# Criss-cross attention and a Fourier mixer: the transform along h by even and odd frequencies, and one more tap by DMA

## The chip, the cores and the metric

The kernel runs on one core of a Trainium2 chip. The metric is the device time of one execution in microseconds (us), lower is better. TensorE is called PE in the profile, its weight loads PEld, VectorE DVE, ScalarE ACT, GpSimd POOL and SyncE SP.

## The reference

The input x has 8 images of 128 by 128 pixels (h, w) with 64 channels, all float32. Layer 0 is criss-cross attention: a pixel attends to its column and to its row with one softmax over both. Layer 1 is a mixer with a two-dimensional Fourier transform, and then a depthwise convolution.

```
Q, K, V = x w_q + b_q, x w_k + b_k, x w_v + b_v            # 8, 8 and 64 channels
att = softmax(concat[energy_H (without itself), energy_W])
x   = gamma * (att_H V + att_W V) + x
h   = ln(x, g1, b1) w_te + b_te                            # 64 -> 128 channels
F   = fft2(h, axes=(h, w))
fc  = gelu(concat[Re F, Im F] w_fc + b_fc)                 # 256 -> 256
x1  = x + (Re ifft2(fc[:128] + i fc[128:])) w_tp + b_tp    # 128 -> 64
h2  = ln(x1, g2, b2) w_fe + b_fe                           # 64 -> 128
d   = gelu(depthwise_conv3x3(h2, w_dw) + b_dw)
out = x1 + d w_fp + b_fp                                   # 128 -> 64
```

Here ln subtracts the mean over the channels and divides by sqrt(var + 0.001).

## The kernel before, in words

The program has two stages, one after the other, which meet in DRAM. All tiles are float32.

**Attention.** An image is worked in eight tasks: four "H" tasks, each 32 columns w with h on the partitions, and then four "W" tasks, each 32 rows h with w on the partitions. Task n of 64 is `tasks[n]`. The loop over n runs a software pipeline: in step n, task n + 1 is turned by PE (`turn`, L348), projected (`queries`, `values`, L362 and L381) and its energies' maxima taken by DVE (L438); task n gets its exponentials from ACT (L444) and its first products with the values (`attend`, L403, copied out of PSUM by ACT in L409); task n - 1 gets the rest. The instructions of each engine run in the order written in this loop. An H task's result goes to `yh`, which PE transposes after the fourth H task (`across`, L584 and L585). A W task's result goes to `yw`, a tile for two W tasks of which there are two: tasks 0 and 1 of an image share one, tasks 2 and 3 the other, and the next image takes them again in turn.

From then on POOL works on a W task. `total` (L522 to L524) adds the two denominators after ACT's weights (`weigh`, L514 to L516); in step n + 2 `combine` merges both results into x (L541, L544) and sends x to DRAM (`x2`, L545). The layer norm of layer 1 begins here too, in `norm_step(n, part)`, which is called four times in each step. Parts 0 and 2 square half of a task's x on ACT (L559) and sum it on DVE (L560), parts 1 and 3 sum the squares (L562), all for the task m = n - 4. For m = n - 5, part 3 computes the inverse root on POOL (L89 to L105), and after every second W task POOL scales x into `yw`, reordered to channels by rows (L574), and a DMA from POOL's queue writes these 64 rows of the image to `xn[b]` in DRAM (L578). `xn[b]` has the layout w, half of the image, channel, row in the half. The last three tasks do these things on DVE and SP instead (`merger`, `store`).

```
                    (nc.sync if m >= N - 3 else nc.gpsimd).dma_start(out=xn[b][:, blk // 2, :, :], in_=z)
```

**Mixer.** `transforms(b)` and `mlp(b)` only add tasks to a planner, `Plan`. It has for every task an engine, a cost, what it comes after, buffers that it takes and frees ("slots", of which "mm" are four PSUM banks), and a due time; going through time with the costs, it gives to each engine the ready task that is due first. The steps of the instruction streams of PE, ACT, DVE and POOL are then in that order. Image b is due one `PERIOD` after image b - 1, so that the transforms of image b stand between the instructions of the convolution of image b - 1.

The transforms of an image are these. `along_w` (L798) multiplies each half of `xn` with the real table of the transform along w; the first 64 partitions of its result hold the rows of the first half, the others those of the second, and ACT keeps it in `at` (L807). `along_h(g)` (L816 to L823) transforms along h for a group of four frequencies of w (the list `GROUPS`, 17 groups): four matmuls for one frequency, each with 64 channels as weights, 128 rows as contraction and the 128-wide tables `cos`, `sin` or `nsin` as the moving side. They fill one PSUM bank, and ACT copies it to `f` in one instruction (`keep_h`, L828). `channels` (L838) applies w_fc, `bend` (ACT, L848) the gelu, `hermite` (POOL, L854) adds or subtracts, `project` (L878) applies w_tp, ACT keeps the result in `gt` (L887). `inverse_h` (L893 to L896) and `inverse_w` (L906) go back, and DVE adds to x (L914).

The convolution goes by 17 chunks k of 8 lines, the last of one line. POOL scales the lines (`xc`, L1039), PE turns them (L1073) and expands them (L1095), ACT keeps `h` (L1115). The nine taps of the 3 by 3 window are added in `acc`: ACT makes the first (L1130); some others are made as products by ACT (L1134, tile `pr`) and added by a DMA that accumulates (`gather`, L1138, issued on POOL's queue: pr<-pr adds a second product to the first, acc<-pr adds the sum to `acc`); DVE does the rest as a scalar_tensor_tensor each (`tap`, L1144). Then gelu by ACT (L1191), w_fp by PE (L1206), the add by DVE (L1211) and the store. How many products go by DMA is set here; even chunks have one and odd chunks two, and the last image has one in its even chunks, while its odd chunks are done as full matmuls (`pairs`, L1156).

```
PRODS = 3
BY_DMA, BY_DMA_LAST = (1, 2), 1
```

## Time and profile before

| | us |
|---|---|
| median of 3 runs | 3202.73 |
| lowest and highest | 3199.78, 3213.37 |
| the profiled execution, time | 3198.24 |
| its span, first to last instruction | 3196.4 |
| busy in the span: PE, PEld | 2915.1, 2144.6 |
| busy: DVE, ACT, POOL | 2486.9, 2096.0, 1636.0 |
| attention, from the start to the mixer's first matmul | 1275.5 |
| mixer, from there to the end | 1920.9 |

"Busy" is the time in which an engine executes, and overlapping PE instructions are counted once. The span is what the program spends between its first and its last instruction; the profiled execution's own time is 1.8 us more, and it lies 4.5 us below the median. A released wait is named after the instruction that came last by the profile; where several end together, the name may be that of a neighbour. A matmul of float32 leaves two records. Counts of engines over the whole span mix the two stages, so the stages are best read in windows of their own.

### The profile page before, as it was taken

How to read it: one execution, taken by the hardware profiler on the slowest of the kernel's cores; microseconds unless marked ns; L12 is line 12 of the kernel's file. 1: busy time of each engine (PE TensorE's matmuls, PEld its weight loads, DVE VectorE, ACT ScalarE, POOL GpSimd, SP SyncE). 2: the span in 40 equal slices, each digit the busy share in tenths (PEclk: the TensorE clock that was granted, in tenths of full speed). 3: DMA queues.
4: the chain of work that ended last, by engine and by line, in shares of the span. 5: the costliest groups of instructions: out<-in, count | busy, mean ns of one | idle time of the engine just before them, and what ended most of it. 6: DMA issues, size and time to landing. Idle time of an engine off the chain costs nothing.

```text
span 3196.4 us, 110388 instructions
## 1 busy us (share of the span) xinstructions
PE 2915.1 (91%) x50476; PEld 2144.6 (67%) x50476; DVE 2486.9 (78%) x2313; ACT 2096.0 (66%) x2744; POOL 1636.0 (51%) x1974
## 2 busy tenths in 40 slices
PE   7998898988888986999999999999999999999978
PEld 5877777777777776766666575675675675665644
DVE  4575747574747576819999999999999999999996
ACT  3665656565656654537868867767777777777754
POOL 1095959595959585424525516515525425435421
PEclk8999999999999998999999999999999999999989
DMA  6024242424243422242674664655745745745645
GB/s 175 23 96 121 96 130 99 121 95 121 101 132 104 122 95 104 99 159 50 134 172 89 157 144 85 170 117 93 182 105 108 176 96 111 178 94 100 120 90 100
DMA packets 227069, 372.71 MB, mean 117 GB/s; under 512 B 143401, under 2 KB 176812, under 8 KB 208044
## 3 DMA queue, kind: packets, MB, share of 16 engines
q0 software_dynamic: 37072, 188.39, 26.1%
q1 hardware_dynamic: 188764, 177.19, 19.7%
q8 instruction: 396, 6.49, 0.8%
q14 instruction: 69, 0.57, 0.1%
q10 hardware_dynamic: 768, 0.07, 0.0%
HBM read 170.96 MB, written 102.26 MB: 85 GB/s over the span
## 4 chain that ended last, share of the span: by engine, by line
PE 49%; DVE 29%; POOL 9%; issue 6%; DMA 4%; ACT 2%; SPq 0%; POOLq 0%; ACTq 0%; DVEq 0%
DVE acc L1144 16%; PE fcps L838 6%; PE yp L403 6%; PE e L433 4%; PE dps L906 4%; POOL xb L544 3%; PE yps L893 3%; PE yps L895 3%; DVE m L438 3%; PE vps L381 3%; PE tp L348 3%; DMA acc<-pr 3%; PE pq L362 3%; PE op L1206 3%; PE tpy L584 2%
## 5 line engine op out<-in xcount | busy, mean ns | idle before, releaser
L1144 DVE SCALAR_TENSOR_TENSOR acc<-h,pk,acc 128x1024 f32<-128x1024 f32 x840 | 1270.0, 1517 | 49.6 <-ACT acc L1130 28.1
L854 POOL TENSOR_TENSOR gs<-gl 128x512 f32<-128x512 f32 (+2 forms) x272 | 441.9, 1644 | 303.3 <-ACT gl L848 301.9
L838 PE MATMUL fcps<-f,pk 128*128 128x512 f32 (+2 forms) x1088 | 508.9, 598 | 0.2 <-ACT f L828 0.2
L438 DVE TENSOR_REDUCE m<-e 128x8 f32<-128x1024 f32 x256 | 300.6, 1211 | 211.5 <-PE e L433 211.3
L444 ACT ACTIVATE att<-e 128x1024 f32<-128x1024 f32 x256 | 259.7, 1024 | 170.2 <-PE e L433 166.3
L848 ACT ACTIVATE gl<-fcps,pk 128x1024 f32<-128x1024 f32 (+2 forms) x272 | 289.9, 1073 | 96.3 <-PE fcps L838 77.6
L1039 POOL TENSOR_TENSOR xc<-x,st 128x512 f32<-128x512 f32 x128 | 184.1, 1454 | 293.8 <-PE tpn L1073 117.1
L1138 POOL DMA_DIRECT2D acc<-pr x120 | 105.6, 880 | 443.4 <-DVE acc L1144 268.6
L403 PEld LDWEIGHTS yp<-v,att 128*64 128x64 f32 x8192 | 268.9, 143 | 87.3 <-issue 39.6
L433 PE MATMUL e<-kt,qt 32*128 32x128 f32 x4096 | 302.7, 291 | 25.4 <-DVE v L384 13.6
L838 PEld LDWEIGHTS fcps<-f,pk 128*128 128x128 f32 x1088 | 191.9, 193 | 196.2 <-issue 146.4
L403 PE MATMUL yp<-v,att 128*64 128x65 f32 x8192 | 296.8, 229 | 18.9 <-issue 17.3
L433 PE MATMUL e<-qt,kt 32*128 32x128 f32 x4096 | 300.1, 288 | 12.2 <-issue 10.1
L433 PEld LDWEIGHTS e<-kt,qt 32*128 32x128 f32 x4096 | 262.6, 194 | 38.1 <-DVE v L384 17.6
L433 PEld LDWEIGHTS e<-qt,kt 32*128 32x128 f32 x4096 | 258.6, 193 | 19.7 <-issue 13.1
L820 PE MATMUL fps<-tb,at 128*64 128x128 f32 x1008 | 200.4, 281 | 23.3 <-DVE ot L1211 23.3
L1134 ACT ACTIVATE pr<-h,pk 128x1024 f32<-128x1024 f32 x176 | 214.3, 1237 | 0.0
L878 PEld LDWEIGHTS gps<-pk,gs 128*64 128x64 f32 x4032 | 137.3, 144 | 108.7 <-issue 57.5
L1115 ACT ACTIVATE h<-hp,pk 128x512 f32<-128x512 f32 x254 | 156.4, 669 | 71.4 <-PE hp L1095 71.2
L384 DVE TENSOR_TENSOR v<-vps,bv 128x1024 f32<-128x1024 f32 x128 | 156.0, 1218 | 60.6 <-PE vps L381 60.6
L893 PE MATMUL yps<-tb,gt 128*64 128x128 f32 x1024 | 202.0, 279 | 0.6 <-ACT gt L887 0.6
L894 PE MATMUL yps<-tb,gt 128*64 128x128 f32 x1024 | 202.0, 279 | 0.0
(218 smaller groups left out, 7419.9 us busy)
## 6 DMA issues: line engine op xcount, KB each, us to landing
acc<-pr POOLq DMA_DIRECT2D x120, 512.0 KB, 5.4
xb<-in_x_dram SPq DMA_DIRECT2D x32, 1024.0 KB
xn<-xn SPq DMA_DIRECT2D x32, 1024.0 KB
x<-x SPq DMA_DIRECT2D x32, 1024.0 KB
x<-spread POOLq DMA_DIRECT2D x32, 1024.0 KB, 8.4
x<-xb POOLq DMA_DIRECT2D x30, 1024.0 KB, 4.9
out_dram<-ot SPq DMA_DIRECT2D x120, 256.0 KB
xn<-yw POOLq DMA_DIRECT2D x14, 2048.0 KB, 9.4
```

The lines of the kernel that those rows point to most:

```text
L403: nc.tensor.matmul(yq[z, q, j, :], lhsT=att[:, q, j, z], rhs=self.v[:, r, :], start=True, stop=True)
L433: nc.tensor.matmul(e[:, q, j, :], lhsT=left[rows, 4 * a + j, :], rhs=right[rows, 4 * a + j, :], start=not msk, stop=j == 3 or not msk,)
L438: nc.vector.tensor_reduce(new.mneg[:, 2 * k : 2 * k + 2, 4 * a : 4 * a + 4], e1, AX.X, ALU.max, negate=True,)
L444: nc.scalar.activation(att, e2, AF.Exp)
L820: nc.tensor.matmul(fps[0:64, n, :], lhsT=re, rhs=cos, start=True, stop=False)
L838: nc.tensor.matmul(ps[:, sgn, 0:n], lhsT=w[:, cols], rhs=fv, start=True, stop=not mean)
L848: nc.scalar.activation(gl[:, :, 0:n], ps[:, :, 0:n], AF.Gelu, bias=bfc[:, half : half + 1])
L854: nc.gpsimd.tensor_tensor(gs[:, 0:n], gl[:, 0, 0:n], gl[:, 1, 0:n], ALU.add if half == 0 else ALU.subtract)
L893: nc.tensor.matmul(yps[0:64, c, :], lhsT=gr, rhs=cosn, start=True, stop=False)
L894: nc.tensor.matmul(yps[64:128, c, :], lhsT=gi, rhs=cosn, start=True, stop=False)
L1134: nc.scalar.activation(pr, self.lines(k, t), AF.Identity, bias=zero, scale=wdw[:, t : t + 1])
L1144: nc.vector.scalar_tensor_tensor(out=a, in0=self.lines(k, t), scalar=wdw[:, t : t + 1], in1=a, op0=ALU.mult, op1=ALU.add)
```

## The change

The halves of an image are no longer stored as they are. `xn[b]` gets in its first half the sum and in its second the difference of rows h and h + 64. The first two W tasks of an image are written to both halves by one DMA whose source repeats. After the other two, two DMAs add them to the first half in DRAM, and ACT makes the negative in four parts (tile `zn`, three buffers), each of which a DMA adds to the second half. For the last image DVE forms both, and SP writes them.

In the mixer the even frequencies of h then need only the sums and the odd ones only the differences, each with 64 rows. `along_h` takes two groups of frequencies at once and works on 64 partitions at a time with tables 64 wide: eight matmuls for one frequency, in two PSUM banks, one for even and one for odd frequencies of h. ACT copies each bank's part by itself. The tables `cos`, `sin` and `nsin`, the offsets in `project` and the tables of the way back follow the new order of frequencies.

Besides, in every chunk but the small ones of all images but the last, two products go by DMA (before: in odd chunks), with four `pr` buffers for three; the calls of `norm_step` with parts 0 to 2 stand later in the step; ACT in place of DVE copies an H task's maxima (L481); and the planner's due times and costs have other values.

```
-PRODS = 3
-BY_DMA, BY_DMA_LAST = (1, 2), 1
-
-
-PERIOD, GROUP0, GROUP, BACK0, BACK = 262.0, -1.9, 10.3, 174.8, 4.3
-CHUNK0, CHUNK, STAY, LOADX = 18.2, 14.2, 0.1, -10.2
+PRODS = 4
+BY_DMA, BY_DMA_LAST = (2, 2), 1
+PERIOD, GROUP0, GROUP, BACK0, BACK = 265.1, -5.4, 9.7, 171.9, 4.7
+CHUNK0, CHUNK, STAY, LOADX = 16.0, 14.4, 0.1, -18.5
+ZN = 3
+DLAG, LATE = 6.9, 8.6
+AH = 0.33
...
-    full = 2.0 * np.pi * (np.outer(n, n) % P) / P
+
+    k = np.arange(64)
+    half = 2.0 * np.pi * np.concatenate([np.outer(k, 2 * k + z) % P for z in range(2)], axis=0) / P
+    freq = np.concatenate([2 * k, 2 * k + 1])
+    full = 2.0 * np.pi * (np.outer(freq, n) % P) / P
...
-    out = np.concatenate([rw, cos, sin, -sin, cos / P, sin / P, -sin / P, idw], axis=1)
+    out = np.concatenate(
+        [rw, cos / P, sin / P, -sin / P, idw, np.cos(half), np.sin(half), -np.sin(half)], axis=1
+    )
...
-TBL_W = 8 * P
+TBL_W = 5 * P + 3 * 64
...
             if way == "H":
-                nc.vector.tensor_copy(o.mh[:, cols].rearrange("p (q i) -> p q i", q=4), s.mneg)
+                nc.scalar.copy(o.mh[:, cols].rearrange("p (q i) -> p q i", q=4), s.mneg)
...
                 if part == 3 and blk % 2 == 1:
-                    z = s.yw.rearrange("p r c -> p (r c)")[:, 0 : 2 * R * C].rearrange("p (c r) -> p c r", c=C)
+                    z = packed_lines(m)
                     for o, lo in ((state[m - 1], 0), (s, R)):
                         for h in range(0, R, 8):
                             merger(m).tensor_tensor(
                                 z[:, :, lo + h : lo + h + 8].rearrange("p c r -> p r c"), o.xb[:, h : h + 8, :],
                                 o.t[:, 0, h : h + 8].unsqueeze(2).to_broadcast([P, 8, C]), ALU.mult,
                             )
-                    (nc.sync if m >= N - 3 else nc.gpsimd).dma_start(out=xn[b][:, blk // 2, :, :], in_=z)
+                    if m < N - 3 and blk == 1:
+                        nc.gpsimd.dma_start(out=xn[b], in_=z.unsqueeze(1).to_broadcast([P, 2, C, 2 * R]))
+                    elif m < N - 3:
+                        for c in (slice(0, 32), slice(32, C)):
+                            nc.gpsimd.dma_start(out=xn[b][:, 0, c, :], in_=z[:, c, :], accum_op=ALU.add)
+                    elif blk == 3:
+                        z0 = packed_lines(m - 2)
+                        nc.vector.tensor_tensor(z0, z0, z, ALU.subtract)
+                        nc.vector.scalar_tensor_tensor(out=z, in0=z, scalar=2.0, in1=z0, op0=ALU.mult, op1=ALU.add)
+                        nc.sync.dma_start(out=xn[b][:, 0, :, :], in_=z)
+                        nc.sync.dma_start(out=xn[b][:, 1, :, :], in_=z0)
+            m = n - 6
+            if is_w(m) and tasks[m][2] == 3 and m < N - 3 and part:
+                for c in ((0,), (1,), (2, 3))[part - 1]:
+                    c = slice(16 * c, 16 * c + 16)
+                    zn = late.tile([P, 16, 2 * R], F32, tag="zn", name="zn", bufs=ZN)
+                    nc.scalar.mul(zn, packed_lines(m)[:, c, :], -1.0)
+                    nc.gpsimd.dma_start(out=xn[tasks[m][0]][:, 1, c, :], in_=zn, accum_op=ALU.add)
...
                 if new is not None:
                     new.queries()
-                norm_step(n, 0)
                 if last is not None:
...
                 flush(1)
-                norm_step(n, 1)
                 if is_w(n - 2):
                     invert(n - 2)
                 if new is not None or old is not None:
                     for k in range(2):
                         energies(0, k, new, old, masked)
-                norm_step(n, 2)
+                norm_step(n, 0)
                 if is_w(n - 1):
                     weigh(n - 1)
                 if new is not None:
                     new.values(1)
+                norm_step(n, 1)
                 if old is not None:
                     target(n)
                     old.attend(0, 1, old.y)
@@ -646,6 +675,7 @@
                 if new is not None or old is not None:
                     for k in range(2):
                         energies(1, k, new, old, masked)
+                norm_step(n, 2)
                 if is_w(n - 1):
                     total(n - 1)
                 norm_step(n, 3)
...
-        rw, cos, sin, nsin, cosn, sinn, nsinn, idw = (tb[:, P * i : P * i + P] for i in range(8))
+        rw, cosn, sinn, nsinn, idw = (tb[:, P * i : P * i + P] for i in range(5))
+        cos, sin, nsin = (tb[:, 5 * P + 64 * i : 5 * P + 64 * i + 64] for i in range(3))
...
-            def along_h(self, g):
+            def along_h(self, gs):
+
 
                 at = self.at.rearrange("p (k t) c -> p k t c", t=2)
-                fps = ps_m.tile([P, 4, P], F32, tag="mm", name="fps")
-                for n, k in enumerate(g):
+                fps = [ps_m.tile([P, 8, 64], F32, tag="mm", name="fps") for _ in range(2)]
+                rows = (slice(0, 64), slice(64, 128))
+                for n, k in enumerate(k for g in gs for k in g):
                     if k % 64 == 0:
-                        a = at[:, 0, k // 64, :]
-                        nc.tensor.matmul(fps[0:64, n, :], lhsT=a, rhs=cos, start=True, stop=True)
-                        nc.tensor.matmul(fps[64:128, n, :], lhsT=a, rhs=nsin, start=True, stop=True)
+                        for ps, r in zip(fps, rows):
+                            a = at[r, 0, k // 64, :]
+                            nc.tensor.matmul(ps[0:64, n, :], lhsT=a, rhs=cos[r, :], start=True, stop=True)
+                            nc.tensor.matmul(ps[64:128, n, :], lhsT=a, rhs=nsin[r, :], start=True, stop=True)
                         continue
-                    re, im_ = at[:, k, 0, :], at[:, k, 1, :]
-                    nc.tensor.matmul(fps[0:64, n, :], lhsT=re, rhs=cos, start=True, stop=False)
-                    nc.tensor.matmul(fps[64:128, n, :], lhsT=im_, rhs=cos, start=True, stop=False)
-                    nc.tensor.matmul(fps[0:64, n, :], lhsT=im_, rhs=sin, start=False, stop=True)
-                    nc.tensor.matmul(fps[64:128, n, :], lhsT=re, rhs=nsin, start=False, stop=True)
+                    for t, (w, v) in enumerate(((cos, cos), (sin, nsin))):
+                        for ps, r in zip(fps, rows):
+                            nc.tensor.matmul(
+                                ps[0:64, n, :], lhsT=at[r, k, t, :], rhs=w[r, :], start=t == 0, stop=t == 1
+                            )
+                            nc.tensor.matmul(
+                                ps[64:128, n, :], lhsT=at[r, k, 1 - t, :], rhs=v[r, :], start=t == 0, stop=t == 1
+                            )
                 return fps
 
-            def keep_h(self, g, fps):
+            def keep_h(self, g, fps, lo):
+
+                n = len(g)
                 f = pf.tile([P, 4, P], F32, tag="f", name="f", bufs=3)
-                nc.scalar.copy(f[:, 0 : len(g), :], fps[:, 0 : len(g), :])
+                fv = f.rearrange("p k h -> p (k h)")[:, 0 : n * P].rearrange("p (z k h) -> p z k h", z=2, k=n)
+                for z in range(2):
+                    nc.scalar.copy(fv[:, z, :, :], fps[z][:, lo : lo + n, :])
                 return f
...
-                            o = j * P + zo
+                            o = 64 * j + len(g) * zo
...
             for i, g in enumerate(GROUPS):
                 n = len(g)
                 t = t0 + GROUP0 + GROUP * i
-                s, fs, hold = Slot("mm"), Slot("f"), {}
-                p = plan.add(
-                    "PE", 0.47 * n if i else 0.5, lambda g=g, hold=hold: hold.update(ps=im.along_h(g)), keeps, t, "C", (s,)
-                )
-                im.last_h.append(p)
+                fs, hold = Slot("f"), {}
+                if i % 2 or i == 0:
+
+                    gs, pair, banks = (GROUPS[i : i + 2] if i else GROUPS[0:1]), {}, (Slot("mm"), Slot("mm"))
+                    along = plan.add(
+                        "PE", AH * sum(map(len, gs)) if i else 0.5, lambda gs=gs, pair=pair: pair.update(ps=im.along_h(gs)),
+                        keeps, t, "C", banks,
+                    )
+                    im.last_h.append(along)
+                second = i > 0 and i % 2 == 0
                 f = plan.add(
-                    "ACT", 0.1 + 0.12 * n, lambda g=g, hold=hold: hold.update(f=im.keep_h(g, hold["ps"])), [p], t + 1,
-                    takes=(fs,), frees=(s,),
+                    "ACT", 0.3 + 0.12 * n, lambda g=g, hold=hold, pair=pair, lo=4 * second: hold.update(
+                        f=im.keep_h(g, pair["ps"], lo)), [along], t + 1,
+                    takes=(fs,), frees=banks if second or i == 0 else (),
                 )
...
                     by_dma = 0 if small else BY_DMA_LAST if last else BY_DMA[k % 2]
-                    late = 0 if last else 6 * by_dma
+                    late = 0 if last else LATE * by_dma
...
                             made = plan.add(
-                                "POOL", 1.0, lambda k=k, n=n: m.gather(k, n, 1), [a, made], t + 6 * n - 5, frees=(s,), lag=7.0
+                                "POOL", 1.0, lambda k=k, n=n: m.gather(k, n, 1), [a, made], t + 6 * n - 5, frees=(s,), lag=DLAG
...
                         g = plan.add(
-                            "POOL", 1.0, lambda k=k: m.gather(k, 1), [g, made], t + late + 4, frees=(slot,), lag=7.0
+                            "POOL", 1.0, lambda k=k: m.gather(k, 1), [g, made], t + late + 4, frees=(slot,), lag=DLAG
```

## The prediction

> **What bounds the kernel now.** I read the page's slices first, then windows cut at the kernel's own periods, then the chain of waits, then single rows. The slices show two stages: up to slice 16 the attention stage with POOL alternating between 9 and 5 tenths, and from slice 17 on the mixer, in which PE and DVE both stand at 9.
>
> ```profile
> PE   7998898988888986999999999999999999999978
> DVE  4575747574747576819999999999999999999996
> ACT  3665656565656654537868867767777777777754
> POOL 1095959595959585424525516515525425435421
> ```
>
> Mixer. In the chain the pieces of L798 that begin an image's transform come at 2136.50 and 2365.10: a period of 229 to 231 us. The windows cut there say what fills it (columns: length, then busy us of PE, weight loads, DVE, ACT, POOL, then granted clock, DMA share, GB/s).
>
> ```profile
> 1905.80:2136.50 230.70, 217.47 (x2620) 147.47 (x2621) 214.11 (x190) 173.04 (x231) 101.29 (x80) 0.97 0.59 129
> 2136.50:2365.10 228.60, 217.04 (x2620) 147.06 (x2620) 213.33 (x190) 172.97 (x231) 101.99 (x80) 0.97 0.60 130
> ```
>
> PE and DVE are both within 16 us of the period: taking work from only one of them would leave the other, so the reader should ask what the change takes from both. ACT has 57 us to spare.
>
> Attention. An image takes 155 us, PE is busy for about 139 of them and POOL for 113, so neither is full on the average. The chain of waits around the change of image shows a loop through both:
>
> ```profile
> 253.41 7.15 POOL yw L574 x7
> 260.85 9.54 DMA xn<-yw
> 270.49 0.60 ACT yw L409
> 271.14 3.79 PE e L433 x60
> ```
>
> POOL normalises the first half of image 0 into the buffer `yw`, a DMA writes it out, and only when it has landed may ACT copy the next image's first vertical result into that buffer; PE waits behind. In the timeline the next steps are fixed: POOL starts to combine that image at 315.5 (it waits 12.2 us for ACT's weights of the following block), works without a gap until it issues the same DMA at 414.82, and ACT's copy again begins at 424.37, at its landing. So the loop is 44 us of PE steps, 100 us of POOL and 9.5 us of DMA, 154 us, which is the period. The seven issues (260.85, 414.82, 570.42, 724.55, 879.91, 1034.88, 1187.40) are 152.5 to 155.6 us apart, and ACT or PE stands 4 to 7 us before each landing. What is added to this DMA is added to the image.
>
> **What the skill says.** The Trainium skill, "TensorEngine Tiling (Array Packing)", Tiling Modes: a 64×64 configuration has four independent tiles. The trace agrees: L381, already 64×64 with 64 columns, issues 64 records in 1.09 us (170.65 to 171.74), 17 ns each, while L820 to L823 (128×64, 128 columns) take 55 ns each (pairs 0.109 us apart). "SBUF — State Buffer", Who interferes with whom: a DVE instruction with two SBUF inputs and a GpSimd one that reads SBUF exclude each other for a whole instruction. L1144 agrees: many taps of 1.09 us, others of 2.19, mean of the large ones 1.60. "DMA: Bandwidth & Descriptors", Issuing engines are not separate DMA queues: all DMAs share the same 16 engines. While the DMA above moves, the DMA share is 1.05 at 333 GB/s with a load beside it, so twice the bytes cannot hide in idle DMA engines.
>
> **The change, part by part.**
>
> ```profile
> 2011.30 0.32 PE L820 MATMUL fps<-tb,at 128*64 128x128 f32 x1
> ...
> 2013.20 1.13 PE L1095 MATMUL hp<-xtn,pk 64*128 64x512 f32 x4
> ...
> 170.65 1.16 PE L381 MATMUL vps<-wv,xt 64*64 64x64 f32 x64
> 171.74 0.38 PE L433 MATMUL e<-kt,qt 32*128 32x128 f32 x2
> ```
>
> *Transform along h.* Now one frequency is 4 matmuls, 8 records (each f32 matmul leaves two) at 55 ns: 0.437 us; the group of four above takes 1.75 of the 1.90 between its lines. After, it is 8 matmuls, 16 records, of the shape of L381: 16 × 17 = 0.272 us. 63 frequencies × 0.165 = 10.4 us of PE for each image. Bounds: a quarter of 55 ns per record (half the columns, twice the tiles at once) gives 13.7; a change of tile shape at every call, and PSUM held for two groups at once (two of four "mm" buffers), can take back 3. I take 10.4.
>
> *Copies of the result.* ACT's one 512-wide copy (590 ns) becomes two of 256; L1108, 256 wide, takes 416 ns. 16 × (832 − 590) = 3.9 us more ACT for each image.
>
> *Second product in even chunks.* In 7 images 8 chunks each give one DVE tap to ACT and DMA: 56 taps. A tap is worth 1.09 (alone) to 1.60 us (mean): 8.7 to 12.8 us of DVE for each image. ACT gains 8 × 1.237 = 9.9; POOL 8 issues of pr<-pr × 0.936 = 7.5 us; the 16 DMA engines 8 × 512 KB, at 128 packets of 340 ns over 16 engines 2.7 us each, 22 us on 0.59 × 230 = 136. POOL (101 of 230) and DMA have room; a later sum of a chunk is absorbed by four `acc` buffers, and `pr` gets a fourth. The added wait is POOL's, for the landing of pr<-pr before acc<-pr; behind it queue the sums `gs` that PE's projection needs. It occurs now in odd chunks, four times in five periods, 15.1 us in all (3.4 us of PE at 2065); doubled it costs PE some 3 us a period at most.
>
> *Together.* In a mixer period PE goes from 217 to 207, DVE from 214 to about 203, ACT from 173 to 187, POOL to 109. With today's gaps kept the period would fall by 10.4. I take 8.7, since that wait and ACT at 187 of 221 delay more of what PE needs. Seven images overlap in this way: 7 × 8.7 = 61 us. Image 0's transform runs alone with PE 79 of 80 us busy: 10.4. The tail of image 7 has no transform and keeps one product. Sum: **71 us saved** (7 × 4 + 8 = 36 to 7 × 11 + 12 = 89). The reordered tasks of the planner (new due times) I cost at nothing, between −10 and +10: its priorities move work among gaps of 13 us a period.
>
> *Sums and differences.* The first DMA of an image now writes the block twice, 4 MB for 2. In the packet records its 128 packets of 16 KB fill 6.4 us (262.17 to 268.53). Another 128 cost 5.2 (650 ns each over 16 engines) to 9 (a 1 MB load that now comes right behind shares the engines). I take 6.0; as the loop shows, all of it counts: 7 × 6.0 = 42 us lost. The second half: two accumulating DMAs and four of the negative, in all 4 MB read, added and written in DRAM. No row of before accumulates into DRAM; the nearest, into SBUF, moves 512 KB in 2.7 us of packets and lands in 5.4. At that pace 2 MB of sums take 11 us, and the buffer is not wanted before 315.1, 33 us after the issue at 281.8: hidden. The six issues (0.9 each for one before) fall into POOL's idle 282.7 to 314.3; the first of them must wait for the doubled DMA, which lands 16 us after its own issue, while this one comes 21 after. Their ACT part is 4 × 1.05 us in the block after the change of image, inside the 44 us that PE bounds; ACT is 60% busy over an image, and behind it queue the copies of `yp` and `xt` that PE needs: 0 to 4 us, I take 1: 7 us.
>
> *Reordered norm, copy to ACT.* Squares and sums (1.06, 1.21 us) and the 0.57 us copy are moved later or off DVE in the horizontal blocks. They shorten PE's way there, but PE already arrives 4 to 7 us early at the landing, so the cover is that stall and I count 0; if the loop were not binding they could give 1 us a block, 28 in all. The last image's two 4,096-wide DVE operations (about 4 × 1.09 each) delay the loads of x from 1358.6 to some 1373; the first add of the mixer comes after 1403 (1393 with a shorter transform): hidden, at worst 5.
>
> **Sum** on the profiled execution (span 3196.4, time 3198.2, 4.5 below the median 3202.7): 3198 − 71 + 42 + 7 = **3176 us**. A measurement of this kernel tells about 0.5%, 16 us, from no change: the borders are 3187 and 3219.
>
> **Rivals.** (1) *The loop does not bind*: the stall before each landing is only where PE would wait anyway. For it: POOL and PE have idle time in every image, and in two of seven changes of image the trace blames PE. Against: the copy starts at the landing to 0.1 us in the others, and POOL then has no gap for 100 us. Time 3198 − 71 = 3127. (2) *ACT becomes the mixer's bound*: for it, ACT reaches 83 of 100 us between 2200 and 2300 already, and gets 14 us a period; against, it is 57 us below the period on the average. The period falls by 4 alone: 3198 − 28 − 10 + 49 = 3209. (3) *Slower: accumulating into DRAM holds ACT.* The fourth negative needs a buffer of three back, so it waits until the first negative's DMA has landed, behind 2 MB of sums. At the pace of SBUF that is just in time (the sums end at 21 + 11 = 32 us after the first DMA's issue, the first negative some 6 after its own issue at about 38, and the fourth is wanted at about 44). If DRAM is half as fast or slower, ACT stands in the loop, and PE behind it. From 6 us an image (7 × 6 = 42) the kernel is slower than before by over 0.5%; at 10 us it takes 3246. Nothing in the trace prices such a DMA, which is what speaks for it. (4) That the new matmuls do not run four at a time is nearly excluded by L381.
>
> **Numbers.** Main case 0.45, own range 3155 to 3197; (1) 0.12; (2) 0.23; (3) 0.20. Faster by over 0.5%: 0.35 of the main case, all of (1), 0.02 of (2): 0.49. Within: 0.10 + 0.15 + 0.02 = 0.27. Slower: 0.06 of (2) and 0.18 of (3): 0.24. The range 3122 to 3236 leaves out the lower part of (1) and the far part of (3).
>
> **What would show it.** Right: vertical-block changes 160 to 163 us apart, with the first xn DMA landing in 15 to 17 us and ACT's `yw` copy at its landing; mixer period 219 to 223; L381's 17 ns in the new matmuls; DVE near 203 a period. Wrong: attention's period still 155 (rival 1) or beyond 167 with ACT waiting for `zn` (rival 3); a mixer period over 225 with ACT over 90% (rival 2).

## The result, and the profile after

The change makes the kernel slower: 3281.8 us (median of 5 runs, 3279.3 to 3297.8) against 3202.8 us; the ratio of the times is 1.025, with a 95% interval of 1.0225 to 1.0278. The prediction was 3176 us, with a range of 3122 to 3236. The profiled execution of the changed kernel took 3297.8 us (span 3296.0), 16 us above its median, so single stages below may be some us long.

The starts of `along_w` cut the span into stages: attention up to the first, image 0's transform (no convolution beside it), the six mixer periods of images 1 to 6, and a tail with image 7. The experiments are in the table too; each row is one profiled execution, in us. Rows with the same code in a stage show what one profile is worth: the nine profiles with the attention code of e2_copy_half gave 1272 to 1290 (mean 1283), the four with that of before 1275.5 to 1278.7 (mean 1277); in the six periods the four with the mixer of the changed kernel (after, e1, e2, g2) gave 1383.1 to 1393.2, so less than 10 us in that column says little by itself. The profile of h2_old_spread is the fastest of its 20 runs, 15.5 us below their median.

```
                     attention  image 0  six periods   tail    span
before                 1275.5    168.7     1372.6     379.6   3196.4
after                  1313.5    206.3     1393.2     383.0   3296.0
e1_zn_last             1313.1    172.5     1383.1     382.4   3251.2
e2_copy_half           1282.7    172.3     1387.3     383.4   3225.7
e3_one_product         1311.6    169.6     1464.8     382.6   3328.6
e4_before_two          1278.7    168.2     1397.4     387.5   3231.8
f1_old_order           1281.7    172.5     1407.6     385.3   3247.0
f2_transform_alone     1272.0    171.4     1395.1     389.7   3228.3
f3_two_new_order       1275.9    168.6     1374.8     374.8   3194.1
f4_longer_lag          1285.6    171.6     1466.9     403.5   3327.6
g1_old_in_pairs        1277.9    167.7     1384.0     378.3   3207.9
g2_split_tail          1282.2    160.3     1383.6     375.9   3202.0
g3_single_groups       1282.4    161.0     1376.2     372.1   3191.7
g4_norm_alone          1267.4    167.8     1377.0     376.4   3188.6
h1_loads_spread        1290.0    160.1     1360.4     372.2   3182.7
h2_old_spread          1258.9    169.5     1368.1     375.2   3171.8
h3_after_spread        1285.1    171.3     1391.9     376.9   3225.2
k1_all_spread          1285.0    160.6     1375.5     374.6   3195.7
```

Of the 99.6 us more in the span of after, attention has 38.0, image 0's transform 37.6, the six periods 20.6, the tail 3.4. The prediction had +49 for attention, −10.4 for image 0's transform and −8.7 for each period: 52 for these six, and once more for image 7, whose transform lies in the tail.

The slices of after's page show the same two stages; new is the hole at the seventeenth, where PE falls to 4 tenths.

```profile
PE   7998979898888886499889999898899898898978
DVE  4574747474747566705888889889799898798896
ACT  3665656565555655255877878778778778778754
POOL 1095959595958685232543524525515425435321
```

Attention first, in after's timeline: POOL's DMA that writes the first half's lines twice, and ACT's next copy into `yw`.

```profile
261.64 0.73 POOL L592 DMA_DIRECT2D xn<-yw  x1 [0.30 <-POOL yw L587]
276.49 1.09 ACT L417 COPY yw<-yp 128x520 f32<-128x520 f32 x2 [12.87 <-DMA xn<-yw]
```

The copy starts 14.85 us after the issue (before: 9.64), again at the landing; ACT stands 12.87 us for it. The seven issues are on the average 159.4 us apart (261.64 to 1218.06; before: 154.4).

Then image 0's transform: rows of after's waits from 1313 to 1520 (engine, line, what it waited for: us in all, times, longest), and windows of the hole (columns as in the prediction).

```profile
POOL gs L895 <- DVE yw L587: 53.5, 1, 53.5
PEld gps L913 <- POOL gs L895: 42.8, 2, 38.2
```

```profile
1340.00:1345.00 5.00, 0.43 (x2) 0.00 (x0) 4.86 (x11) 0.00 (x0) 0.00 (x0) 1.00 0.08 30
1345.00:1350.00 5.00, 0.00 (x0) 0.00 (x0) 4.76 (x13) 0.00 (x0) 0.00 (x0) 0.51 0.00 2
1385.00:1390.00 5.00, 5.00 (x8) 2.02 (x7) 0.00 (x0) 1.65 (x3) 0.78 (x1) 0.56 0.64 234
1390.00:1395.00 5.00, 5.00 (x42) 2.51 (x41) 0.00 (x0) 2.87 (x3) 3.03 (x3) 1.00 0.93 382
```

POOL's first sum `gs` of the mixer waits, once, until DVE has normalised the last image of attention; PE stands 38 us behind it. The granted clock (third column from the end) falls to 0.5 within 5 us of PE's stop; from 1385 to 1390 PE is full again and has 0.56.

Last the mixer: two periods of after.

```profile
1980.20:2212.00 231.80, 209.20 (x3136) 136.00 (x3134) 202.49 (x182) 182.25 (x255) 99.89 (x88) 0.96 0.68 147
2212.00:2448.30 236.30, 210.29 (x3136) 136.97 (x3134) 202.74 (x182) 181.97 (x255) 96.83 (x88) 0.96 0.67 144
```

PE's work fell from 217 to 210 us, DVE's from 214 to 203, as the prediction had them within 3 us, and yet the period did not fall. What grew is idle time: on PE from 12.7 to 22.6 us a period (here and below, means and sums over five periods are of those that begin with images 2 to 6).

### The profile page after: what moved, and what is told of

It reads as the page before. It is cut to its first block, busy times and chain, and to the rows that moved or that the text cites. A ratio compares the mean times of both kernels' runs of the same rounds, so it can differ in the third digit from the quotient of the medians.

```text
span 3296.0 us, 119060 instructions
## 1 busy us (share of the span) xinstructions
PE 2881.9 (87%) x54572; PEld 2073.0 (63%) x54572; DVE 2378.2 (72%) x2227; ACT 2187.6 (66%) x2996; POOL 1661.0 (50%) x2065
## 5 line engine op out<-in xcount | busy, mean ns | idle before, releaser
L1191 DVE SCALAR_TENSOR_TENSOR acc<-h,pk,acc 128x1024 f32<-128x1024 f32 x784 | 1181.8, 1512 | 151.0 <-ACT acc L1177 133.4
L895 POOL TENSOR_TENSOR gs<-gl 128x512 f32<-128x512 f32 (+2 forms) x272 | 415.9, 1545 | 306.6 <-ACT gl L889 227.3
L879 PE MATMUL fcps<-f,pk 128*128 128x512 f32 (+2 forms) x1088 | 527.7, 618 | 15.1 <-ACT f L869 15.0
L441 PE MATMUL e<-kt,qt 32*128 32x128 f32 x4096 | 309.7, 293 | 14.1 <-issue 8.6
L1086 POOL TENSOR_TENSOR xc<-x,st 128x512 f32<-128x512 f32 x128 | 172.3, 1366 | 239.0 <-PE tpn L1120 67.8
L1181 ACT ACTIVATE pr<-h,pk 128x1024 f32<-128x1024 f32 x232 | 278.8, 1234 | 0.0
L919 PE MATMUL gps<-pk,gs 128*64 128x64 f32 x4032 | 160.7, 234 | 70.3 <-DVE ot L1258 42.3
L934 PE MATMUL yps<-tb,gt 128*64 128x128 f32 x1024 | 205.7, 284 | 8.2 <-ACT gt L928 8.2
L955 DVE TENSOR_TENSOR x<-dps,x 128x512 f32<-128x512 f32 x128 | 87.9, 687 | 165.1 <-PE dps L947 165.1
L935 PE MATMUL yps<-tb,gt 128*64 128x128 f32 x1024 | 205.6, 284 | 0.0
```

Source lines behind the costliest of these rows:

```text
L441: nc.tensor.matmul(e[:, q, j, :], lhsT=left[rows, 4 * a + j, :], rhs=right[rows, 4 * a + j, :], start=not msk, stop=j == 3 or not msk,)
L879: nc.tensor.matmul(ps[:, sgn, 0:n], lhsT=w[:, cols], rhs=fv, start=True, stop=not mean)
L895: nc.gpsimd.tensor_tensor(gs[:, 0:n], gl[:, 0, 0:n], gl[:, 1, 0:n], ALU.add if half == 0 else ALU.subtract)
L919: nc.tensor.matmul(gps[z, j, t, :], lhsT=src[:, o : o + 64], rhs=wtp, start=True, stop=True)
L934: nc.tensor.matmul(yps[0:64, c, :], lhsT=gr, rhs=cosn, start=True, stop=False)
L935: nc.tensor.matmul(yps[64:128, c, :], lhsT=gi, rhs=cosn, start=True, stop=False)
```

## The experiments

Every kernel has the edit shown and nothing else; the numbers are read against the table above. Times are medians; the ratio is to before.

**The hole in image 0's transform.** In both kernels the mixer opens the pool of `gs` last. The change takes zn's 12 KB from a pool opened early in attention, ahead of the pool with the last image's lines, which move up by as much. In this run zn gets a pool that is opened after that of the lines:

```
+        negs = ctx.enter_context(tc.tile_pool(name="a_neg", bufs=ZN))      # after a_xw
-                    zn = late.tile([P, 16, 2 * R], F32, tag="zn", name="zn", bufs=ZN)
+                    zn = negs.tile([P, 16, 2 * R], F32, tag="zn", name="zn")
```

> After, with the three negated chunks zn in a pool of their own that is opened after the pool of the last image's lines, so that the lines keep the addresses that they have in before; nothing else is changed. Theory 1, overlap: zn's 12 KB in the pool of late buffers pushed the lines of the last image up into the addresses of the mixer's sums gs, and POOL's first sum waits for the last image's VectorE operation to have read those lines (53.5 us, one time in after). Then this wait goes, image 0's transform takes 165 to 172 us instead of 206, the rest stays, and the time falls by 35 to 45 us, to 3237 to 3247. Theory 2, late inputs: the wait is there because the last image's two VectorE operations of 4096 (4.4 and 4.8 us) and the two writes behind them come late in any layout, so that image 0's transform starts late wherever the lines lie. Then the transform still takes over 195 us and the time falls by less than 10 us. Attention's period of 160 us and the mixer's of 232 us stay in both.

Measured: 3253.1 us (1.0185, 1.0166 to 1.0205), 29 us less than after; image 0's transform 172.5 instead of 206.3, with the wait for DVE gone; the time fell by 6 us less than the band of theory 1, the stage by what it said. So the 34 us were a wait between two buffers that have nothing to do with each other but their address (no trace shows addresses; that these two overlap follows from the order of the pools, and from the wait being gone when only that order changes).

**The loop of attention.** On e1_zn_last, the first write goes to one half only, and a copy from memory to memory fills the other later:

```
+                    if m < N - 3 and blk == 3:            # part 3, ahead of the products
+                        nc.gpsimd.dma_start(out=xn[b][:, 1, :, :], in_=xn[b][:, 0, :, :])
-                        nc.gpsimd.dma_start(out=xn[b], in_=z.unsqueeze(1).to_broadcast([P, 2, C, 2 * R]))
+                        nc.gpsimd.dma_start(out=xn[b][:, 0, :, :], in_=z)
```

> As e1_zn_last, and the write of the first two blocks' lines goes to one half of xn alone (2 MB as in before, instead of 4 MB); the second half is filled by a copy from memory to memory, issued by GpSimd two steps later, where ScalarE doesn't wait for it. Theory 1, loop: ScalarE's first copy of the next image's lines waits for this write to have read the lines, and a longer write lengthens the loop of attention; then attention's period goes from 160 back to 154 to 156 us, and the time falls by 28 to 42 us against e1_zn_last. Rival: the period of 160 comes from what VectorE, ScalarE and the queue of GpSimd got in addition, the negations and six accumulating writes among them; then it stays over 158 us and the time falls by less than 12 us. A third: the copy takes the engines' time from the accumulating writes behind it, and the last image's outputs come later; then the attention stage is shorter, but image 0's transform longer by some of it.

Measured: 3235.3 us (1.013, 1.0086 to 1.0175), 18 us less than e1_zn_last; attention 1282.7 instead of 1313.1, the issues 154.9 us apart instead of 159.1. Theory 1 for the loop. The time fell by less than the 28 expected; its four times spread over 25 us, and in the profiles the spans are 25.5 apart. The third theory fails: image 0's transform didn't grow.

**One product or two.** One product again in the even chunks, on e1_zn_last; then two in before.

```
e3_one_product                               e4_before_two
-BY_DMA, BY_DMA_LAST = (2, 2), 1             -PRODS = 3
+BY_DMA, BY_DMA_LAST = (1, 2), 1             +PRODS = 4
                                             -BY_DMA, BY_DMA_LAST = (1, 2), 1
                                             +BY_DMA, BY_DMA_LAST = (2, 2), 1
```

> As e1_zn_last, with one product by DMA again in the even chunks (two in the odd ones, as in before). The transform in even and odd frequencies is kept. Theory 1, chain of accumulating writes: ScalarE waits in its queue for the second product's two writes to land before it can go on to the next chunk's taps and to the evictions; the mixer's period then falls from 232 to 222 to 228 us with one product less, and the time by 25 to 60 us against e1_zn_last, although VectorE gets some 9 to 12 us an image back. Rival A: VectorE's work binds and the longer period has another cause (the due times by which the order of the queues is made, or the four banks shared by the transform's matmuls); then the period rises or stays, 231 to 240 us, and the time stays or grows by up to 50 us. Rival B: neither; within 6 us of e1_zn_last.

> Before, with two products by DMA in every chunk and four buffers of products instead of three; the transform along h, the attention and the constants of the order stay those of before. Theory 1, chain of accumulating writes: this alone makes the mixer's period longer than before's 230 us by 3 to 10 us, so the time grows by 20 to 70 us over before, with ScalarE's waits at its bends for the writes (18.5 us over five periods in before) going to over 50. Rival A: the second product relieves VectorE (214 us of 230) and the period falls to 220 to 226 us, the time by 30 to 70 us; then it is the transform along h or the constants that cost the period in after. Rival B: within 12 us of before.

e3_one_product took 3331.9 us (1.0434, 1.0404 to 1.0465), 79 us more than e1_zn_last: rival A, more than its bound. e4_before_two took 3231.1 us (1.0109, 1.0083 to 1.0135), 35 us more than before: the time of theory 1, with ACT's waits for the writes at 60.4 us over five periods. So the second product costs in before's setting and gives in that of after. Neither theory covers both; what differs between the settings is the transform and the planner's due times.

**Transform, products, order, one at a time.** f1_old_order is e2_copy_half with the due times and delays of before; f2_transform_alone is that with one product and three buffers; f3_two_new_order is e4_before_two with the due times and delays of after; f4_longer_lag is e2_copy_half with a longer delay of the gathers.

```
f1, f2 (f3 the other way)
-PERIOD, GROUP0, GROUP, BACK0, BACK = 265.1, -5.4, 9.7, 171.9, 4.7
-CHUNK0, CHUNK, STAY, LOADX = 16.0, 14.4, 0.1, -18.5
-DLAG, LATE = 6.9, 8.6
+PERIOD, GROUP0, GROUP, BACK0, BACK = 262.0, -1.9, 10.3, 174.8, 4.3
+CHUNK0, CHUNK, STAY, LOADX = 18.2, 14.2, 0.1, -10.2
+DLAG, LATE = 7.0, 6.0
f4
-DLAG, LATE = 6.9, 8.6
+DLAG, LATE = 11.0, 8.6
```

> As e2_copy_half (new transform, two products in every chunk), with the planner's due times and delays set back to those of before (PERIOD 262.0, GROUP0 -1.9, GROUP 10.3, BACK0 174.8, BACK 4.3, CHUNK0 18.2, CHUNK 14.2, LOADX -10.2, delay of a gather 7.0, LATE 6.0). In e2_copy_half six periods of the mixer took 1387 us (before 1373). Theory 1: the order is part of the cause; the due times of after suit neither load; then six periods come to 1345 to 1372 us and the time falls by 15 to 42 us. Theory 2: the new transform or the second product costs the period whatever the order; then 1380 to 1400 and the time stays within 12 us. Theory 3: the new due times are what the two parts need; then over 1410, the time at least 25 us longer.

> As f1_old_order with one product in the even chunks and three buffers of products, as in before: of the change in the mixer only the transform along h is left. e3_one_product, which differs from this in the due times, the delays and the fourth buffer, took 1465 us for six periods. Theory 1 (my prediction's step): PE loses 10 us a period, VectorE keeps its 214; six periods come to 1330 to 1373 us. Theory 2: the transform in pairs of groups, which takes two of the four PSUM buffers at once and one copy more on ScalarE, delays the projection and the evictions, and the 92 us that e3_one_product lost are its own; then over 1430. Theory 3: half is the order's; 1380 to 1430.

> As e4_before_two (old transform and attention, two products in every chunk), with the due times and delays of after. e4_before_two took 1397 us for six periods, 25 more than before. Theory 1: the later due times of the chunk's end (LATE 8.6 for 6.0) are what lets two products' writes land in time; then six periods come to 1355 to 1380 us and the time falls by 17 to 42 us against e4_before_two. Theory 2: a second product costs the period through ScalarE's queue whatever the order; then 1390 to 1410, the time within 12 us. Theory 3: the new due times fit the new transform alone; then over 1415.

> As e2_copy_half, with the planner's delay of a gather (what it reckons from its issue to the landing) at 11.0 us instead of 6.9; nothing else is changed, so that only the order in the queues can differ. Theory 1, chain of writes: ScalarE stands at its bend for a write that lands later than planned (56 to 60 us over five periods, 14 times, up to 9.7), with taps and evictions behind it; reckoned with 11.0 the bend is put behind them, that wait falls below 25 us and six periods from 1387 to 1350 to 1375. Rival: the waits for landings are a consequence of other delays and not their cause; the wait falls or not, and six periods stay within 10 of 1387 or grow.

Times: 3252.9 (1.0167, 1.014 to 1.0193), 3230.1 (1.0093, 1.0067 to 1.0118), 3198.1 (0.9996, 0.9982 to 1.0011) and 3322.9 us (1.0382, 1.0358 to 1.0406). The six periods of all:

```
                         order of before   order of after
old transform, one            1372.6             –
old transform, two            1397.4          1374.8
new transform, one            1395.1          1464.8
new transform, two            1407.6          1387.3
```

ACT's waits for the writes, in e4_before_two and f3_two_new_order, then in e2_copy_half and f4_longer_lag:

```profile
ACT acc L1191 <- DMA acc<-pr: 60.4, 28, 5.2
ACT acc L1191 <- DMA acc<-pr: 64.8, 25, 5.2
ACT acc L1241 <- DMA acc<-pr: 57.0, 14, 8.6
ACT acc L1241 <- DMA acc<-pr: 18.6, 6, 5.3
```

Three things follow. The new transform costs 10 to 23 us in every pair that differs in it, where 62 (six times 10.4) were to be gained on PE: neither order saves it (f1 lies between its theories 2 and 3; f2 is theory 3). With the old transform the second product gives nothing even in the order of after (f3: 2 us from before, with DVE at 198 us a period instead of 214). f3 has the number of theory 1, but not its mechanism: its writes don't land in better time, ACT waits for them as long as in e4. And the order is worth more than either: with the one delay at 11.0 (f4), ACT's waits for the writes fell from 57.0 to 18.6 us as theory 1 had it, but the six periods grew by 80. So shorter waits for the writes did not make a shorter period; the rival stands. What these waits cost in e2 itself f4 doesn't show, as the one delay moves the whole order.

**Why the new transform costs.** PE's waits over five periods, before and then e2_copy_half:

```profile
PE fps L820 <- DVE ot L1211: 19.4, 5, 3.9
PE gps L878 <- POOL gs L854: 15.7, 10, 3.4
PE gps L878 <- DVE ot L1211: 14.8, 7, 2.9
PE op L1206 <- ACT acc L1191: 8.9, 8, 1.4
```

```profile
PE gps L922 <- DVE ot L1261: 35.8, 10, 5.8
PE op L1256 <- ACT acc L1241: 12.3, 5, 3.5
PE fcps L882 <- ACT f L872: 11.6, 18, 1.3
PE tpn L1123 <- ACT f L872: 11.3, 5, 2.4
PE gps L922 <- POOL gs L898: 11.1, 12, 1.4
```

The rows that name `f` are new, 22.9 us together: PE's turn of lines (`tpn`) waits for a PSUM buffer that the transform's pair still holds, and `fcps` for ACT's two copies. The wait for DVE's add (`ot`) is not: it has 34.2 us in two rows in before and 35.8 in e2. g1_old_in_pairs puts this holding and copying on the old matmuls (f3_two_new_order with two groups at a time in two "mm" buffers, two copies of 256 each); g3_single_groups goes the other way, with the new matmuls planned for one group and both buffers free after it. g2_split_tail, its base, is e2_copy_half with the last image's two DVE operations cut. The edits of g1, g3 and g2, in this order:

```
+                two = [ps_m.tile([P, 4, P], F32, tag="mm", name="fps") for _ in range(2)]
+                for m, k in enumerate(k for g in gs for k in g):
+                    fps, n = two[m % 4 // 2], m // 4 * 2 + m % 2
...
+                for z in range(len(g) // 3 + 1):
+                    n = min(2, len(g) - 2 * z)
+                    nc.scalar.copy(f[:, 2 * z : 2 * z + n, :], fps[z][:, lo : lo + n, :])
```

```
-                if i % 2 or i == 0:
+                if True:
-                    gs, pair, banks = (GROUPS[i : i + 2] if i else GROUPS[0:1]), {}, (Slot("mm"), Slot("mm"))
+                    gs, pair, banks = GROUPS[i : i + 1], {}, (Slot("mm"), Slot("mm"))
-                second = i > 0 and i % 2 == 0
+                second = False
...
-                    takes=(fs,), frees=banks if second or i == 0 else (),
+                    takes=(fs,), frees=banks,
```

```
-                        nc.vector.tensor_tensor(z0, z0, z, ALU.subtract)
-                        nc.vector.scalar_tensor_tensor(out=z, in0=z, scalar=2.0, in1=z0, op0=ALU.mult, op1=ALU.add)
+                        for c in (slice(8 * c, 8 * c + 8) for c in range(8)):
+                            u, v = z0[:, c, :], z[:, c, :]
+                            nc.vector.tensor_tensor(u, u, v, ALU.subtract)
+                            nc.vector.scalar_tensor_tensor(out=v, in0=v, scalar=2.0, in1=u, op0=ALU.mult, op1=ALU.add)
```

> As f3_two_new_order (old matmuls of the transform along h, attention of before, two products, the order of after; six periods 1374.8 us), but the transform along h goes over two groups at a time into two PSUM buffers of four, each with two frequencies of either group, both held until the second group is copied, and each group is copied in two halves of 256: the buffers and copies of the changed kernel with the matmuls of before. Theory 1, buffers: what the new transform costs is this hold and these copies (PE waits for VectorE's add to give a buffer back: 38.2 us in f2_transform_alone, 35.8 in e2_copy_half); then six periods come to 1390 to 1425 us and the time is 15 to 50 us longer than f3_two_new_order. Rival: the hold costs nothing, and the gain was lost because the mixer's period is set by something else than PE's work; then six periods stay within 8 us of 1374.8.

> As e2_copy_half, with the last image's two VectorE operations of 4096 each cut into eight of 512, in turn; the same work. In e2_copy_half image 0's transform takes 172.3 us, PE stands there some 6 us for two sums of GpSimd that took 5.4 us instead of 1.27 while the two operations ran, and 2.6 us more later. Theory 1, lock: a VectorE operation with two inputs in SBUF shuts GpSimd out for its whole length; in pieces the sums slip between; no sum takes over 2.6 us, and the transform 160 to 167 us. Rival: the pieces shut it out as long in all, or PE's work there isn't what sets the end; then 170 to 175. The mixer's periods stay as in e2_copy_half, and the time falls by 5 to 12 us or by less than 3.

> As g2_split_tail, with the new transform along h planned for one group at a time: it still takes two PSUM buffers, but holds them until that group is copied instead of two groups. Theory 1, buffers: half the hold gives back a part of what the transform costs; six periods fall from 1387 to 1360 to 1378 us, and the waits of PE for VectorE's add below 20 us over five periods. Rival A: twice as many starts with two buffers to be had at once wait twice as often; over 1395. Rival B: PE's buffers are not what binds; within 8 us of 1387.

g1_old_in_pairs: 3206.1 us (1.002, 1.0004 to 1.0035), 8 us more than f3_two_new_order, at the edge of the noise; six periods +9.2, between theory 1's 15 and the rival's 8. Holding and copying cost some 8 us without any new matmul; e2_copy_half is within the noise of it, so its shorter matmuls gave nothing back. g3_single_groups: 3195.5 us (0.9993, 0.998 to 1.0007), 17 us less than g2_split_tail; PE's waits for DVE's add fell from 35.3 to 5.0 us. Those are the numbers of theory 1, but other waits took their place: five periods of g2, then of g3, and g3's longest row of PE's waits (1.1 us in g2).

```profile
1667.50:2826.10 1158.60, 1047.10 (x15666) 686.50 (x15664) 1009.30 (x906) 909.52 (x1275) 493.97 (x440) 0.96 0.68 147
1671.60:2819.60 1148.00, 1032.57 (x15666) 674.24 (x15664) 1003.42 (x906) 911.68 (x1275) 513.77 (x440) 0.97 0.68 148
PE dps L952 <- ACT ys L947: 40.6, 5, 8.9
```

PE's idle time (length less busy time) is 111.5 and 115.4 us, no shorter. What fell is its busy time, by 14.5 us for the same matmuls, and with it the time at half clock, 96 and 68 us. So the shorter hold let PE run faster and did not let it wait less. g1 has the same the other way: against f3 PE is idle for 75.2 us instead of 73.2, but busy for 1081.6 instead of 1074.5.

g2_split_tail: 3212.5 us (1.0039, 1.002 to 1.0058), 23 us less than e2_copy_half. The profiles put 12.0 of it in image 0's transform, as theory 1 had it, and 7.5 in the tail and 3.7 in the six periods, where the edit changes nothing: that part is not explained. The timeline of e2_copy_half shows what was there, DVE and then POOL; below, the row of the sums in g2_split_tail (min, median and max ns).

```profile
1355.85 4.42 DVE L601 TENSOR_TENSOR yw<-yw 128x4096 f32<-128x4096 f32 x1
1360.31 5.37 DVE L602 SCALAR_TENSOR_TENSOR yw<-yw 128x4096 f32<-128x4096 f32 x1
```

```profile
1356.52 11.51 POOL L898 TENSOR_TENSOR gs<-gl 128x512 f32<-128x512 f32 x3 [4.29 <-ACT gl L892]
```

```profile
L900 POOL TENSOR_TENSOR gs<-gl x23: 997/1275/2257, 1333.3 to 1394.2; 128x512 f32<-128x512 f32 x22, 128x384 f32<-128x384 f32 x1
```

Three sums of 1.27 us took 11.51 (the longest 5.44) while the two operations ran, and PE stood 6.1 us for them and 2.2 soon after. In pieces no sum takes over 2.26, and these stalls are gone: the lock, as the Trainium skill has it ("SBUF — State Buffer", Who interferes with whom: the shared ports are an exclusive lock); a long instruction makes a long lock.

**The reordered norm alone**, in before (and the copy of the maxima on ACT as in the change's diff):

```
-                norm_step(n, 0)                      # ahead of last.attend
-                norm_step(n, 1)                      # ahead of invert
-                norm_step(n, 2)                      # ahead of weigh
+                norm_step(n, 0)                      # ahead of weigh
+                norm_step(n, 1)                      # behind new.values(1)
+                norm_step(n, 2)                      # behind energies(1, ...)
```

> Before, with only norm's parts moved later in the horizontal blocks and the copy of the negated maxima on ScalarE, as in after. My prediction's step: it costs and gives nothing, as PE arrives 4 to 7 us before the landing that binds; attention 1270 to 1280 us (1275.5 in before), the time within 8 us of before. Rival: VectorE's earlier targets shorten PE's way; attention 1247 to 1265, the time 10 to 28 us shorter.

3191.0 us (0.9971, 0.9961 to 0.9982): 8 us less than before, and the profile has it in attention (1267.4; h2_old_spread below, with the same attention, 1258.9). Between the two expectations, and nearer to the first: the reordering gives 0.3%.

**What holds the period.** With PE's work at 206.5 us a period in g3_single_groups and DVE's at 201, the period is that of before. One stall stands out, once in each period: PE 8.9 us at 1838.7, 8.4 at 2068.0, 8.2 at 2297.0. ACT, DVE and POOL in the timeline of g3_single_groups there:

```profile
2074.80 1.06 ACT L1243 ACTIVATE acc<-acc 128x1024 f32<-128x1024 f32 x1 [7.02 <-DMA acc<-pr]
```

```profile
2078.50 0.69 DVE L960 TENSOR_TENSOR x<-dps,x 128x512 f32<-128x512 f32 x1 [6.36 <-PE dps L952]
```

```profile
2078.00 0.88 POOL L1190 DMA_DIRECT2D acc<-pr  x1 [11.36 <-DMA pr<-pr]
```

ACT waits for a write issued at 2064.85, which lands some 9.9 us later (the median is 4.9); POOL waits 11.36 for the one behind it. At 2052.3 the next image's four loads of `xn` went out together and at 2061.4 one of x, 5 MB in all. f3_two_new_order has a like stall (39.4 us in five periods). h1_loads_spread issues the second to fourth load from ACT's queue about a chunk apart:

```
+                on_act = n > 0 and older is not None
+                if on_act:
+                    after = after + [older.done[8 + n]]
-                normed.append(plan.add("SP", 1.0, lambda n=n: im.load_normed(n), after, t0 - 40 + n, lag=14.0))
+                normed.append(plan.add(
+                    "ACT" if on_act else "SP", 0.1 if on_act else 1.0,
+                    lambda n=n, q=nc.scalar if on_act else nc.sync: im.load_normed(n, q), after, t0 - 40 + n, lag=14.0))
```

h2_old_spread has the same in f3_two_new_order with the reordered norm, h3_after_spread in e2_copy_half; in k1_all_spread the first load moves too (`on_act = older is not None`, on g3_single_groups as h1).

> As g3_single_groups, with the second to fourth of the next image's four loads of xn (1 MB each) issued from ScalarE's queue one chunk apart instead of all at once from SyncE's. In g3_single_groups the four loads and one of x come within 10 us once in each period; the accumulating writes then take 10 us instead of 5.4 to land, ScalarE stands 7 us for one of them, and PE 7 to 9 us behind it (40.6 us in five periods). Theory, collision: that is what keeps the period at 229 us although PE has 206 and VectorE 201 us of work; spread, this stall falls below 3 us, six periods from 1376 to 1325 to 1355 us, and the time by 20 to 50 us. Rival A: another wait takes its place at once; PE's stall is gone, but six periods stay within 12 us of 1376. Rival B: the late write isn't the loads' doing; the stall stays.

> As f3_two_new_order (old transform, two products, order of after) with the reordered norm of g4_norm_alone and the loads of xn spread as in h1_loads_spread. f3_two_new_order has the same stall of PE once a period (39.4 us in five, behind ScalarE). Theory, collision: that stall goes; PE's 215 us of work then bind; six periods 1330 to 1362 instead of 1374.8, attention 1265 to 1272, and the time 3145 to 3180. Rival A: another wait takes its place; six periods within 10 us of 1375 and the time 3183 to 3197.

> As e2_copy_half (transform in pairs of groups, two products, order of after), with the loads of xn spread as in h1_loads_spread. Its stalls of PE are many smaller ones (2 to 4 us, for GpSimd's sums, VectorE's adds and ScalarE's copies) and none of 8 us. Theory, collision alone: six periods fall from 1387 by 20 us or more. Rival, buffers: the hold of two PSUM buffers over two groups is this kernel's own limit; six periods stay within 12 us of 1387.

> As h1_loads_spread, with the first of the four loads of xn put on ScalarE's queue too, so that none of them goes out when the transform's last matmul is done. h1_loads_spread has half of the stall left (4 to 5 us once a period, 23.2 in five). Theory, collision: what is left comes from the first load and the load of x that follows; the stall falls below 3 us and six periods from 1360 to 1335 to 1352 us. Rival: what is left isn't the loads' doing; six periods stay within 8 us of 1360, or grow if the first load now comes close to the first use.

h1_loads_spread: 3178.5 us (0.9942, 0.9927 to 0.9958), 17 us less than g3_single_groups. Its row of PE's waits shows half of the stall left:

```profile
PE dps L952 <- ACT ys L947: 23.2, 5, 5.3
```

The six periods fell by 15.8 us, between the theory (21 at least) and rival A (12 at most); 10.4 of it lie in the first of them, while the five in which the stall was counted fell by 5.4 and the stall by 17.4. Nor do the writes land sooner: in these periods acc<-pr takes 9.9 us at most in g3_single_groups and 10.2 in h1_loads_spread, and of 95 in six periods 8 and 15 take over 7 us. ACT only stands less for a late one (38.0 and 23.6 us). So spreading the loads gives 17 us, but that these came from writes landing in time is not shown.

h2_old_spread: 3189.1 us (0.9971, 0.9956 to 0.9986), no clear gain over the 3191.0 of g4_norm_alone, which has the reordered norm too. Its stall fell from 39.4 to 14.4 us, and another row of 16.8 came (`dps`, behind ACT's `ys`): rival A. h3_after_spread: 3226.2 us (1.0109, 1.0059 to 1.016), six periods 4.6 more than e2_copy_half: no gain, as the rival had it, so in the changed kernel itself the loads cost nothing that shows. k1_all_spread: 3191.1 us (0.9975, 0.9961 to 0.9989), 13 more than h1_loads_spread: the rival's number, but not for its reason, as no `along_w` waits for a load there.

What keeps h1's period at 228 us on the average, with PE at 208 and DVE at 201, is open; its longest row of PE's waits has 29 us in 25 pieces. f3_two_new_order and g3_single_groups have the same six periods (1374.8 and 1376.2) with PE busy for 215 and 207 us of each: PE's work alone is not what sets them. The chain of waits can be followed through the periods in a few runs only. There the landings of pr<-pr and acc<-pr are 6.0% of five periods in before, 10.4 in f2_transform_alone, 12.7 in e4_before_two and 17.2 in f1_old_order, but 2.8 in f4_longer_lag, whose periods are the longest: they are not the whole of it either. No run set the planner's due times anew for the lighter work.

h1_loads_spread is the best of the kernels tried, 0.6% faster than before, of which the reordered norm, which gave 0.3% alone, may be half. It is the change with zn's pool moved, the first write halved, the last image's operations cut, one group at a time, and the loads spread.

## Why the prediction was wrong, step by step

Against the prediction, the span is 122 us too long: attention is 11 us better than it had, image 0's transform 48 worse, the six periods 73 and the tail 12.

*The loop of attention* was right in mechanism and sign. Writing the lines twice was put at 6.0 us an image, 42 in all. The landing came 5.2 us later in image 0, and halving the write, with the copy beside it, took off 29.7 us in all (mean of three profiles with the doubled write, 1312.7, against the nine of 1283), 4.2 an image: a term that measured 30 for 42. (The packets of before's write, which the prediction reads as ending at 268.53, run to 269.8 in the trace; its sum doesn't use this.) How much of these 5.2 us is off the path was not tried. Negatives and sums were put at 7, the reordered norm at 0; together, with e2's copy, they measure +6 (1283 against 1277). That is near by luck: the norm alone gives 8, so if the terms add, which no run tried, the writes and the copy cost about 14. Rival 3 had the sign of the result, slower, but not the cause: in after a negative's write lands in 5.4 to 9.3 us, and though an image's sums take 13 to 18 us where 11 were put, ACT never waits for `zn`.

*The last image's two operations, "hidden, at worst 5"*: this step failed, by 46 us (206.3 against 160.3). It looked only at the data they delay. In place of the 5 the runs show 34 us for an overlap of addresses (e1_zn_last), which comes from the place of `zn` and for which the prediction had no term at all, and 12 for GpSimd shut out while the two long operations run (g2_split_tail). With both taken away the transform alone takes 160.3 us, 8.4 less than before, close to the 10.4 of the prediction: the price of the matmuls was nearly right, and this stage was in fact PE's.

*"With today's gaps kept the period would fall by 10.4. I take 8.7"*: this step failed, by 73 us over six periods, 12 in each. The terms on each engine were right (PE 210 for 207, DVE 203 for 203, ACT 182 for 187); the assumption that the gaps stay was not. PE's gaps grew by 10 us a period, and its time at half clock from 68 to 106 us in five. If busy time at half clock is counted as half (an estimate from the trace's clock records: PE is busy for 62 of these 68 us and for 94 of the 106), PE's work fell by 9.9 us a period, about the 10.4 of the prediction. The gaps took all of that, and the slower clock some 3 us more.

Why the gaps grew is shown in small part. Of 49 us more in five periods, rows that name `f`, the held buffers and the two copies, have 23. Holding and copying cost some 8 us in all (g1_old_in_pairs), and halving the hold brought 7 back in six periods and 17 in the time (g3_single_groups). The loads that h1_loads_spread spreads have no part in it: in the changed kernel spreading them gives nothing (h3_after_spread), and it gives 17 only once the hold is halved. The rest is open. The prediction named the held buffers and put them at 3 us at most inside the 10.4. The added wait that it priced, POOL's for pr<-pr, grew as it said (15.1 to 39.7 us in five periods), but PE's waits for `gs` behind it hardly did (15.7 to 17.1).

*Planner's order at 0, between −10 and +10*: under-sized most of all. The changed kernel takes 20 us less over six periods in its own order than in that of before (f1 to e2), and 80 more with one delay changed (f4); the order decides whether a second product costs before 25 us or nothing (e4, f3). So this term did not make the kernel slower, but no other can be sized without it.

*The second product's 8.7 to 12.8 us of DVE* came off DVE and not off the time: with PE at 215 of 229 the other engine's relief has no effect (f3_two_new_order). The prediction asked for work taken "from both"; it got it, and then waits took its place. Rival 2, ACT as the bound, is not shown: ACT works 182 of 232 us.

## What to carry over

When two engines are nearly full and a change relieves both, the busy times tell what could be gained, not what will be: look at which buffers and writes the relieved engines will wait for next, and at what many short waits do to the granted clock. A new buffer can move another to an address where it must wait for a stage that it has nothing to do with, so compare what overlaps at the border of two stages. In a kernel whose queues come from a planner, a new piece of work and the order made for it must be judged together.

## What the runs showed of the hardware

**Gaps on PE cost twice.** The granted clock changes in stretches that are multiples of 3.41 us and is 1.0 or 0.5. The Trainium skill ("TensorE: Matmul & The Clock Gate", What's actually happening) says that the clock is halved after an idle window of that length. Here a window need not be idle: in e2_copy_half and before, from 1460 to 2800 us, the windows ahead of a half-clock stretch had PE busy for 31% and 21% at the median, at most 61% and 45%; no window under 47% was followed by full clock. Over five periods before has 68 us at half clock, e2_copy_half 113 and f4_longer_lag 181, so a part of the work taken from PE was given back as slower matmuls. It also matters where these stretches fall. In f3_two_new_order, with one stall of 8 us in a period, PE is busy in only 21 of its 44 us at half clock; in g1_old_in_pairs, which has short waits instead, in all of its 51.

**Small matmuls were a little cheaper than put.** The new transform's 64×64 matmuls with 64 columns run four in 58 ns, 14.5 ns a record, where the prediction took 17 from L381.
